# Eleven of twenty tile transposes from TensorE to VectorE and DMA, in a two-layer kernel

## The chip, the cores and the metric

One Trainium2 chip; the kernel runs on one of its cores. The metric is the device time of one execution in microseconds. Three runs of the kernel before took 754.48, 754.50 and 754.84, median 754.5. The profile is of one further execution of the same program.

## The reference

The input is `x` of shape (4, 512, 256), all in float32. Two layers follow each other; each normalizes and adds two branches to its input:

```python
xn = _layernorm(x, axis=-1)
x = x + _L0_attn_ref(xn, ...) + _L0_ffn_ref(xn, ...)
xn = _layernorm(x, axis=-1)
x = x + _L1_attn_ref(xn, ...) + _L1_ffn_ref(xn, ...)
```

The first branch of layer 0 is an mLSTM block with its own MLP. What matters here is its end (`_rmsnorm(x, w)` is `w * x * rsqrt(mean(x * x) + eps)` over the features):

```python
h_out = jax.nn.sigmoid(o_pre) * h_norm
x1 = x + h_out @ w_out
h2 = _rmsnorm(x1, norm2_w)
mlp = jax.nn.silu(h2 @ w_gate) * (h2 @ w_up) @ w_down
return x1 + mlp
```

The second branch of layer 0 is a gated FFN of 704 columns with eight low-rank experts, of which the router chooses two for each token. Layer 1 has causal attention over the first axis (four positions, 16 heads) and a gated FFN of 1024 columns whose hidden values are thinned to two of four.

## The kernel before, in words

The 512 positions are cut into four row blocks `j` = 0 to 3 of 128. A block with its four batch entries is a tile of 128 partitions by 4 x 256. A product contracts over the partitions, so whatever is multiplied with a weight over its 256 features must first lie with features on partitions: two halves `k` of 128 features, each with 4 x 128 tokens. Each such turn is one "tile transpose": `transposed` does one half `k` with four 128x128 TensorE transposes into a PSUM bank and one ScalarE eviction; a whole tile takes eight transposes and two evictions. Each row block has five of them, 20 in all:

- `front`: the normalized input of layer 0, into `xnT` (for block 0 `first_front` does it in pieces)
- `out`: the gated mLSTM output `sg`, into `hoT` (tile name `featT`), multiplied with `w_out`
- `second`: the second norm's result, into `h2T` (also `featT`); here the eviction multiplies with `norm2_w`
- `norm`: the normalized input of layer 1, in `front_rows`, into `xnT`
- `mixed`: the attention output `o` of layer 1, into `oT`, read by `finish_rows`

Layer 0 runs for each block `front`, `choice` and `routing` (which experts; `low` are the low-rank inputs), `mlstm`, `experts` (matmul outputs `chunk`, `acc`) and `mlp` (outputs `gp`, `up`, then `yp`). Layer 1 runs `attention_rows`, `attend_rows`, `rows` (gate and up as products of a seven-product scheme, outputs `x`, `y`, `z`), `sparsified` and `finish_rows`.

These parts are generators. `Flow` interleaves them into one order while the program is built: a `Clock` holds an estimate of when each engine is free and each tile ready, and a generator that yields a time is continued when TensorE's estimated time has come there. The order so found is kept on every engine (`keep_in_program_order`); DMAs are all issued on SP's queue except for four loads at the start. In this plan a DMA counts 0.5 us for issue, a given time, and 2.0 until it has landed. The program that runs has no planner in it: each engine takes its instructions in that fixed order and waits for semaphores.

`mlstm(0)` scales `w_out` on POOL (GpSimd) before its first use. `inv_sqrt` is a power, also on POOL. In `mlstm` the per-head sums `ss` go through it, then VectorE multiplies `ss` with `den`, then POOL forms `sg` (tile name `qm`) from it with four operations.

All compute instructions go through the wrapper at line 225, so they carry that line in the profile and are told apart by tile names. DMAs carry line 330.

Of the kernel before, what the change touches and what calls it, by code (L numbers as in the profile page):

```python
# [13 lines left out]
P = 128  # L14
# [14 lines left out]
BANKS = 8  # L29
AHEAD = 4  # L30
LITTLE = 1.0


@with_exitstack
def layers_kernel(ctx: ExitStack, tc: tile.TileContext, io: dict, out: bass.AP):
# [440 lines left out]
                xn[:, b, :], x[:, b, :], mv[:, b, 0:1], rstd[:, b : b + 1], ALU.subtract, ALU.mult  # L476
            )

    def transposed(src, dst, k, scale=None):

        pt = mm_ps("pt")
        for i in range(B):
            transpose(pt[:, i * P : (i + 1) * P], src(i, k), ident)
        if scale is None:
            act.copy(dst[:, k, :], pt)
        else:
            act.mul(dst[:, k, :], pt, scale[:, k : k + 1])

    def project(ps, w, xT, lo, n):

        for k in range(KD):
            mm(ps[0:n, :], w[:, k, lo : lo + n], xT[:, k, :], start=(k == 0), stop=(k == KD - 1))

# [8 lines left out]
    def sides(w, rooms, by):  # L504
# [12 lines left out]
        def kept(n):  # L517
# [3 lines left out]
                "a22": lambda q: v[:, 1, q, 1, :], "s3": lambda q: v[:, 0, q, 1, :],  # L521
                "s1": kept(0), "s2": kept(1), "s4": kept(2)}

    def other_sides(xT, t, by):

        b11, b12, b21, b22 = (xT[:, k, h * HALF : (h + 1) * HALF] for k in range(2) for h in range(2))
        for n, a, b in ((0, b12, b11), (1, b22, t[:, 0, :]), (2, b22, b12), (3, b21, t[:, 1, :])):
            by.tensor_tensor(out=t[:, n, :], in0=a, in1=b, op=ALU.subtract)
        return {"b11": b11, "b21": b21, "b22": b22,
                **{f"t{n + 1}": t[:, n, :] for n in range(4)}}  # L530

# [87 lines left out]
    def front_rows(j, norm=None):  # L619

        xn = new(both, [P, B, D], "xn")
        yield from norm(x_sb[j], xn) if norm else layernorm(both, x_sb[j], xn)
        xT = new(both, [P, KD, S], "xnT")
        for k in range(KD):
            yield from flow.wait(xn, banks=1)
            transposed(lambda l, k: xn[:, l, k * P : (k + 1) * P], xT, k)
        yield from flow.wait(xT)
        xTs[j] = xT

    with ExitStack() as l0:  # L630
        wk0 = l0.enter_context(tc.tile_pool(name="l0", bufs=1))
# [37 lines left out]
        def front_tiles(j):  # L669
            xns[j] = new(both, [P, B, D], "xn")  # L670

            rrs[j] = new(sm, [P, 4, B], "rr", 2)
            vas[j] = new(wk0, [P, B, H, DV + 1], "va", 2), new(sm, [P, B, 2 * H], "gz", 2)
            return xns[j], rrs[j], *vas[j], new(both, [P, KD, S], "xnT"), new(sm, [P, B, E], "pr")

        def rms_of(rr, ms, va):

# [5 lines left out]
        def values(xnT, b):  # L683
            vp = mm_ps("vp")
            for k in range(KD):
                mm(vp[:, 0:V], xnT[:, k, cols_of(b)], wvg[:, k, :], start=(k == 0),
                   stop=(k == KD - 1))
            return vp

# [5 lines left out]
        def first_front():  # L695

            x = x_sb[0]
            xn, rr, va, gz, xnT, pr = front_tiles(0)
            stats = new(both, [P, B, 6], "stats", 2)
            mv = new(both, [P, B, 2], "mv", 2)  # L700
            rstd = new(both, [P, 2, B], "rstd2")
# [9 lines left out]
            def normed(b):  # L711
                dve.tensor_scalar(
                    xn[:, b, :], x[:, b, :], mv[:, b, 0:1], rstd[:, 1, b : b + 1], ALU.subtract,
                    ALU.mult)
                pt = mm_ps("pt")
                for k in range(KD):
                    transpose(pt[:, k * P : (k + 1) * P], xn[:, b, k * P : (k + 1) * P], ident)
                act.copy(xnT[:, :, cols_of(b)], pt[:, 0 : KD * P].rearrange(
                    "p (k t) -> p k t", k=KD))
                if b == 0:  # L720
                    keep_busy(4)
                    clock.let_go(idle)
# [50 lines left out]
        def front(j):  # L773

            xn, rr, va, gz, xnT, pr = front_tiles(j)
            ms = rr[:, 3, :]
            yield from layernorm(both, x_sb[j], xn, ms)
            inv_sqrt(rr[:, 0, :], ms)  # L780
            for k in range(KD):
                yield from flow.wait(xn, banks=1)
                transposed(lambda i, k: xn[:, i, k * P : (k + 1) * P], xnT, k)
            yield from flow.wait(rr)
            rms_of(rr, ms, va)
            for b in range(B):
                yield from flow.wait(xnT, rr, banks=1)
                vp = values(xnT, b)
                dve.tensor_copy(pr[:, b, :], vp[:, D + 2 * H : V])
                values_read(vp, b, rr, va, gz)  # L790
            xnTs[j] = xnT
            yield from flow.wait(pr)
            yield from choice(j, pr)
# [43 lines left out]
        def mlstm(j):  # L837
# [277 lines left out]
            if first:  # L1115
                for k in range(KD):
                    pool.tensor_scalar(
                        w_out[:, k, :], w_out[:, k, :], mh_c[:, k : k + 1], 0.5, ALU.mult,
                        ALU.mult)
            sg = new(wk0, [P, B, D], "qm")  # L1120
            for bp in range(0, B, 2):
                yield from flow.wait(banks=1)
                o_ps = mm_ps("o_ps")
                for b in (bp, bp + 1):
                    o = o_ps[:, (b - bp) * D : (b - bp + 1) * D]
                    for k in range(KD):
                        mm(o, xnT[:, k, cols_of(b)], w_og[:, k, :], start=(k == 0),
                           stop=(k == KD - 1))
                for b in (bp, bp + 1):
                    act.activation(  # L1130
                        sg[:, b, :], o_ps[:, (b - bp) * D : (b - bp + 1) * D], AF.Tanh,
                        scale=rr[:, 2, b : b + 1])
# [28 lines left out]
                    out=by_head(sg[:, b, :]), in0=hv[:, b, :, :],  # L1161
                    in1=ss[:, b, :].unsqueeze(2).to_broadcast([P, H, DV]), op=ALU.mult)

            hoT = new(wk0, [P, KD, S], "featT", 2)
            for k in range(KD):
                yield from flow.wait(sg, banks=1)
                transposed(lambda b, k: sg[:, b, k * P : (k + 1) * P], hoT, k)
            for bp in range(0, B, 2):
                yield from flow.wait(hoT, banks=1)
                yp = mm_ps("yp")  # L1170
                for b in (bp, bp + 1):
                    for k in range(KD):
                        mm(yp[:, (b - bp) * D : (b - bp + 1) * D], hoT[:, k, cols_of(b)],
                           w_out[:, k, :], start=(k == 0), stop=(k == KD - 1))
                x1 = xn[:, bp : bp + 2, :].rearrange("p b d -> p (b d)")
                dve.tensor_tensor(x1, yp, x1, ALU.add)
# [13 lines left out]
            yield from flow.wait(r2)  # L1190
            for b in range(B):
                act.mul(xn[:, b, :], xn[:, b, :], r2[:, b : b + 1])
            h2T = new(wk0, [P, KD, S], "featT", 2)
            for k in range(KD):
                yield from flow.wait(xn, banks=1)
                transposed(lambda i, k: xn[:, i, k * P : (k + 1) * P], h2T, k, norm2_c)
            yield from flow.wait(h2T)
            h2Ts[j] = h2T

        def add_down(xb, bp, terms):  # L1200

# [77 lines left out]
        def experts(j):  # L1279
# [23 lines left out]
            def products(ps, parts, step):  # L1303


                for m in range(2):
                    for k in range(KD if step == 0 else 1):
                        for r0, half, c in parts:
                            f0, n = FCH[c]
                            o = ps[r0 : r0 + n, m * T : (m + 1) * T]  # L1310
                            if step == 0:
                                mm(o, wguT[:, m, k, f0 : f0 + n], xnT[:, k, here(half)],
                                   start=(m == k == 0), stop=False, at_once=len(parts),
                                   skip_group_check=True)
                            else:
# [175 lines left out]

        def following(j):

            yield flow.soon(30)
            while j >= 2 and j - 2 not in attended:
                yield flow.soon()
            yield from front(j)
# [44 lines left out]
    with ExitStack() as l1:  # L1542
# [4 lines left out]
        def attend_rows(j, q, k, v):  # L1547
# [37 lines left out]
                    o[:, l, :], pd[:, 0:m, :].rearrange("p m c -> p c m"), AX.X, ALU.add)  # L1585
            while j >= 2 and j - 2 not in out_of:
                yield flow.soon()
            oT = new(wk1, [P, KD, S], "oT", 2)
            for k in range(KD):
                yield from flow.wait(o, banks=1)  # L1590
                transposed(lambda l, k: o[:, l, k * P : (k + 1) * P], oT, k)
            outs[j] = oT

        def sparsified(j, hs):

# [41 lines left out]
        def finish_rows(j):  # L1637
# [5 lines left out]

            while len(halves.get(j, ())) < 2 and j < NJ - 1 or j == NJ - 2 and not written:
                yield flow.soon()
            terms = [(oT[:, k, :], aoT[:, k, :]) for k in range(KD)]
            terms += [(a[:, n, :], f_down[:, 4 * i + n, :])
                      for i, a in enumerate(gated[j]) for n in range(4)]

            m = 1 if j == NJ - 1 else 2  # L1650
# [1 line left out]
            for n0, n1 in ((0, 2), (2, 6), (6, 10)):  # L1652
                for lp in range(0, B, m):
# [7 lines left out]
                    for l in range(lp, lp + m):  # L1661
                        yield 0
                        for n in range(n0, n1):

                            mm(yps[lp // m][:, (l - lp) * D : (l - lp + 1) * D],
                               terms[n][0][:, l * P : (l + 1) * P], terms[n][1],
                               start=(n == 0 and l == lp), stop=(n == 9 and l == lp + m - 1),
                               skip_group_check=True)
            out_of.add(j)
# [8 lines left out]
        def attention_rows(j):  # L1678
# [4 lines left out]
            for l in range(B):  # L1683
                for name, lo, n in (("qk_ps", 0 if l else D, 2 * D if l else D), ("v_ps", 2 * D, D)):
                    yield from flow.wait(xT, banks=1)
                    ps = mm_ps(name)
                    for kk in range(KD):
                        mm(ps[:, 0:n], xT[:, kk, l * P : (l + 1) * P], qkvT[:, kk, lo : lo + n],
                           start=(kk == 0), stop=(kk == KD - 1))
                    if lo < 2 * D:  # L1690
                        if l:
# [11 lines left out]

        bs = {}
        sevens = Sevens(room)
        mm(sevens.z, ident, xTs[0][:, 0, :], start=True, stop=True)

        def room_of_sides():
            return new(wk1, [P, 4, HALF], "xd", 2)
# [148 lines left out]
```

## Time and profile before

| what | value |
|---|---|
| median of three runs | 754.5 us (754.48 to 754.84) |
| profiled execution: span from its first to its last instruction | 753.0 us; the page gives no other time of this execution |
| TensorE busy (matmul) | 746.1 us, 99% |
| VectorE busy | 482.1 us, 64% |
| ScalarE busy | 262.2 us, 35% |
| POOL busy | 173.9 us, 23% |
| transposes named `pt` | 160, of one pass each |
| evictions of `pt` | 0.59 us (plain), 0.68 us (with `norm_w`), 128x512 |
| DMA moved | 25.47 MB in 18961 packets |

By stretches, from the trace (us from the span's start; layer 1 begins at about 522):

| stretch | TensorE busy | VectorE | ScalarE | POOL |
|---|---|---|---|---|
| 0 to 60 | 57.50 | 44.59 | 22.02 | 24.28 |
| 60 to 170 | 109.55 | 76.50 | 37.35 | 26.34 |
| 170 to 280 | 109.65 | 67.99 | 32.31 | 25.87 |
| 280 to 400 | 119.76 | 67.82 | 33.61 | 22.04 |
| 400 to 520 | 120.00 | 63.93 | 27.87 | 20.94 |
| 520 to 640 | 119.81 | 85.17 | 69.67 | 40.52 |
| 640 to 753 | 109.87 | 76.15 | 39.39 | 13.93 |

A group's row reads: line, engine, operation, written tile, read tiles, shape, count, then busy us and mean ns of one, then the idle time before and what ended it. PE is TensorE's matmuls, DVE VectorE, ACT ScalarE. Durations of matmuls overlap, so what a matmul occupies is read from the distance between starts.

### The profile page before, as it was taken

To read this page: it belongs to the slowest core of one execution; us is meant where nothing else is said; L and a number is where in the kernel's file an instruction comes from. 1 tells how busy PE (TensorE), PEld (TensorE's weight loads), DVE (VectorE), ACT (ScalarE), POOL (GpSimd) and SP (SyncE) were. 2 spreads that over 40 slices of the span, in tenths; PEclk is the share of its full clock that TensorE was granted. 3 is DMA by queue.
4 is the path that set the end of the run, shared out by engine and by line. 5 is a ranking of instruction groups with operands and counts; after the bars stand their busy time and mean duration, and the time that the engine had idled before them with its cause. 6 is when DMAs were issued, how large, how long until landed. Compare 5 with 4: busy or idle time off the path is not lost.

```text
span 753.0 us, 10208 instructions
## 1 busy us (share of the span) xinstructions
PE 746.1 (99%) x3962; PEld 552.0 (73%) x3962; DVE 482.1 (64%) x1078; ACT 262.2 (35%) x569; POOL 173.9 (23%) x162
## 2 busy tenths in 40 slices
PE   9999999999999999999999999999999999999998
PEld 6787778766578776765777675655777778788887
DVE  5877586775743788644367745343269898698671
ACT  3334133433122433131233221211276874652510
POOL 6230052050132060203112023040141534520000
PEclk9999999999999999999999999999999999999999
DMA  7930000030000030000030210001000000000001
GB/s 237 300 113 0 3 0 1 3 112 0 1 2 1 3 111 1 1 1 1 0 114 1 112 44 14 1 0 56 1 1 0 2 0 1 29 0 29 1 15 42
DMA packets 18961, 25.47 MB, mean 34 GB/s; under 512 B 2784, under 2 KB 12768, under 8 KB 18912
## 3 DMA queue, kind: packets, MB, share of 16 engines
q1 hardware_dynamic: 17824, 24.53, 10.1%
q8 instruction: 31, 0.51, 0.3%
q10 hardware_dynamic: 1088, 0.28, 0.2%
q14 instruction: 18, 0.15, 0.1%
HBM read 22.65 MB, written 2.16 MB: 33 GB/s over the span
## 4 chain that ended last, share of the span: by engine, by line
PE 91%; DVE 6%; POOL 1%; ACT 1%; issue 1%; DMA 0%; POOLq 0%; DVEq 0%
PE chunk L225 18%; PE yp L225 16%; PE acc L225 11%; PE up L225 9%; PE gp L225 7%; PE x L225 6%; PE y L225 3%; PE qk_ps L225 3%; PE pt L225 2%; PE vp L225 2%; PE o_ps L225 2%; PE lp L225 2%; PE z L225 2%; PE v_ps L225 1%; PE qk L225 1%; PE sums L225 1%
## 5 line engine op out<-in xcount | busy, mean ns | idle before, releaser
L225 ACT ACTIVATE sl<-chunk 128x256 f32<-128x256 f32 x132 | 50.5, 383 | 122.3 <-PE chunk L225 106.6
L225 PE MATMUL chunk<-low,lora 128*128 128x256 f32 (+1 forms) x384 | 85.8, 383 | 1.6 <-DVE he_pair L225 1.1
L225 PE MATMUL chunk<-xnT,wguT 128*128 128x256 f32 (+1 forms) x384 | 83.2, 383 | 0.0
L225 PEld LDWEIGHTS chunk<-xnT,wguT 128*128 128x128 f32 (+1 forms) x384 | 64.2, 181 | 20.4 <-issue 8.8
L225 PEld LDWEIGHTS chunk<-low,lora 128*128 128x128 f32 (+1 forms) x384 | 63.7, 181 | 17.1 <-issue 5.1
L225 DVE SCALAR_TENSOR_TENSOR sl<-sl,chunk 128x256 f32<-128x256 f32 x132 | 54.7, 415 | 29.8 <-ACT sl L225 29.3
L225 PE MATMUL gp<-featT,w_gate 128*128 128x512 f32 x128 | 60.3, 593 | 0.0
L225 PE MATMUL up<-featT,w_up 128*128 128x512 f32 x128 | 60.3, 593 | 0.0
L225 PE MATMUL yp<-w_down,hid 128*128 128x256 f32 x256 | 56.6, 379 | 0.0
L225 PE MATMUL yp<-w_gate,hs 128*128 128x256 f32 x256 | 56.2, 379 | 0.0
L225 PEld LDWEIGHTS yp<-w_down,hid 128*128 128x128 f32 x256 | 48.4, 190 | 8.2 <-issue 1.9
L225 PEld LDWEIGHTS yp<-w_gate,hs 128*128 128x128 f32 x256 | 48.6, 190 | 6.6
L225 ACT ACTIVATE tmp<-gp 128x512 f32<-128x512 f32 x32 | 19.1, 597 | 91.3 <-PE gp L225 91.3
L225 DVE SCALAR_TENSOR_TENSOR tmp<-tmp,gp 128x512 f32<-128x512 f32 x32 | 22.0, 687 | 43.1 <-ACT tmp L225 43.0
L225 POOL TENSOR_TENSOR pd<-k,q 128x512 f32<-128x512 f32 (+2 forms) x12 | 27.8, 2321 | 92.0 <-ACT k L225 82.1
L225 POOL TENSOR_TENSOR ss<-ss,mhalf 128x32 f32<-128x32 f32 x4 | 22.0, 5501 | 101.4 <-DVE ss L225 101.4
L225 PEld LDWEIGHTS up<-featT,w_up 128*128 128x128 f32 x128 | 24.1, 190 | 27.6 <-issue 26.5
L225 PEld LDWEIGHTS gp<-featT,w_gate 128*128 128x128 f32 x128 | 24.0, 190 | 27.5 <-issue 26.8
L225 PE MATMUL acc<-WdT,hid 128*128 128x256 f32 (+1 forms) x192 | 41.1, 382 | 0.0
L225 PE MATMUL acc<-tmp,lora 128*128 128x512 f32 x80 | 40.4, 595 | 0.0
L225 PEld LDWEIGHTS acc<-WdT,hid 128*128 128x128 f32 (+1 forms) x192 | 32.8, 189 | 7.5 <-issue 3.2
L225 DVE TENSOR_TENSOR tmp<-chunk,sl 128x256 f32<-128x256 f32 x80 | 33.9, 424 | 2.8
(293 smaller groups left out, 1325.7 us busy)
## 6 DMA issues: line engine op xcount, KB each, us to landing
ct<-m_dram SPq DMA_DIRECT2D x8, 1024.0 KB, 8.0
x<-in_x SPq DMA_DIRECT2D x3, 512.0 KB, 10.0
out<-x SPq DMA_DIRECT2D x6, 256.0 KB, 2.1
w_gate<-in_w_gate SPq DMA_DIRECT2D x1, 1024.0 KB, 6.4
w_up<-in_w_up SPq DMA_DIRECT2D x1, 1024.0 KB, 7.4
w_down<-in_w_down SPq DMA_DIRECT2D x1, 1024.0 KB, 10.3
wguT<-in_f_gate SPq DMA_DIRECT2D x1, 1024.0 KB, 4.7
lora<-in_f_up SPq DMA_DIRECT2D x1, 1024.0 KB, 5.0
```

The costliest lines, as they stand in the source:

```text
L225: return tc.keep_in_program_order(f(*args, **kw))
```

## The change

A set `MOVED` names 11 of the 20 tile transposes. For these, one VectorE instruction turns every 32x32 block of the tile within its 32 partitions and writes the result to the new tile `t`; a DMA writes `t` to a DRAM tile `moved`; four DMAs read it back, one for each quarter of 32 partitions, so that the blocks come to the right partitions. The other nine stay on TensorE. The transposed tile's layout changes from (half, batch entry, token) to (batch entry, half, token) for all 20, and its readers take it through a view. The multiplication with `norm2_w` moves from the eviction into the weights: POOL multiplies `w_gate` and `w_up` with it once, in `mlstm(0)`. `following` waits 15 instead of 30 of the plan's microseconds before it starts the next block's `front`.

```diff
+MOVED = {('front', 1), ('front', 2), ('front', 3), ('mixed', 0), ('mixed', 2), ('mixed', 3), ('norm', 0), ('out', 0),
+         ('out', 1), ('second', 1), ('second', 3)}
...
-    def transposed(src, dst, k, scale=None):
-
-        pt = mm_ps("pt")
-        for i in range(B):
-            transpose(pt[:, i * P : (i + 1) * P], src(i, k), ident)
-        if scale is None:
-            act.copy(dst[:, k, :], pt)
-        else:
-            act.mul(dst[:, k, :], pt, scale[:, k : k + 1])
+    Q = 32
+    NQ = P // Q
+
+    def turned(src, t):
+
+
+        dve.transpose(
+            t.rearrange("p (m q i) -> p m q i", m=NQ, i=Q),
+            src.rearrange("p l (k m i) -> p m (l k) i", m=NQ, i=Q))
+        n = t.shape[1] // NQ
+        moved = new(dram, [NQ * P, n], "moved")
+        dma(moved.rearrange("(m p) x -> p m x", p=P), t.rearrange("p (m x) -> p m x", x=n), 1.6)
+        for m in range(NQ):
+            dma(t[m * Q : (m + 1) * Q, :].rearrange("i (q a j) -> i q a j", a=NQ, j=Q),
+                moved[m * P : (m + 1) * P, :].rearrange("(a i) (q j) -> i q a j", i=Q, j=Q), 0.6)
+
+    def turned_by(what, j, src, t):
+
+        yield from flow.wait(src)
+        if (what, j) in MOVED:
+            turned(src, t)
+            return
+        for l in range(B):
+            if l % 2 == 0:
+                yield from flow.wait(banks=1)
+                pt = mm_ps("pt")
+            for k in range(KD):
+                i = l % 2 * KD + k
+                transpose(pt[:, i * P : (i + 1) * P], src[:, l, k * P : (k + 1) * P], ident)
+            if l % 2:
+                act.copy(t[:, (l - 1) * KD * P : (l + 1) * KD * P], pt)
+
+    def by_token(t):
+        return t.rearrange("p (l k t) -> p k l t", l=B, k=KD)
...
@@ mlstm, for the first block
                     pool.tensor_scalar(
                         w_out[:, k, :], w_out[:, k, :], mh_c[:, k : k + 1], 0.5, ALU.mult,
                         ALU.mult)
+                    for w in (w_gate, w_up):
+                        pool.tensor_scalar(
+                            w[:, k, :], w[:, k, :], norm2_c[:, k : k + 1], None, ALU.mult)
...
@@ mlstm, second norm; the other four places change in the same way
-            h2T = new(wk0, [P, KD, S], "featT", 2)
-            for k in range(KD):
-                yield from flow.wait(xn, banks=1)
-                transposed(lambda i, k: xn[:, i, k * P : (k + 1) * P], h2T, k, norm2_c)
-            yield from flow.wait(h2T)
-            h2Ts[j] = h2T
+            t = turned_tile(wk0, "featT", 2)
+            yield from turned_by("second", j, xn, t)
+            yield from flow.wait(t)
+            h2Ts[j] = by_token(t)
...
@@ following
-            yield flow.soon(30)
+            yield flow.soon(15)
```

## The prediction

> **What bounds the kernel now.** I read the page's busy times and its slices first, then the chain that ended last.
>
> ```profile
> span 753.0 us, 10208 instructions
> ...
> PE 746.1 (99%) x3962; PEld 552.0 (73%) x3962; DVE 482.1 (64%) x1078; ACT 262.2 (35%) x569; POOL 173.9 (23%) x162
> ...
> PEclk9999999999999999999999999999999999999999
> ...
> PE 91%; DVE 6%; POOL 1%; ACT 1%; issue 1%; DMA 0%; POOLq 0%; DVEq 0%
> ```
>
> TensorE is busy in every slice at the full granted clock, and no other engine comes near it. The waits of TensorE itself (columns: total us, times, longest) leave almost nothing:
>
> ```profile
> PE idle L225 <- POOL ident masks.py:199: 1.5, 1, 1.5
> PE chunk L225 <- DVE he_pair L225: 1.1, 2, 0.9
> PE chunk L225 <- DVE ss L225: 0.4, 1, 0.4
> PE pt L225 <- DVE xn L225: 0.3, 1, 0.3
> PE pt L225 <- DVE o L225: 0.2, 1, 0.2
> ```
>
> So TensorE's own work sets the end: what is taken from it is gained one for one, and every wait that it newly meets is lost one for one. What the eight transposes of a tile occupy is seen in the timeline (start, duration, engine):
>
> ```profile
> 474.62 1.04 PE L225 MATMUL pt<-ident,xn 128*128 128x128 f32 x8
> 475.32 1.26 ACT L225 ACTIVATE featT<-pt,norm_w 128x512 f32<-128x512 f32 x2
> 475.50 1.02 PE L225 MATMUL up<-featT,w_up 128*128 128x512 f32 x2
> ```
>
> Eight transposes start at 474.62 and the next matmul at 475.50: 0.88 us, 0.109 each, although one lasts 0.27. They are one pass each; a 128x256 matmul is two passes 0.216 apart, a 128x512 one two passes 0.429 apart.
>
> **The gain.** 11 tiles x 8 transposes x 0.109 = 9.6 us leave TensorE. The upper bound is the pitch averaged with the gaps around transposes, 0.121, which makes 10.6. 22 evictions (0.59 or 0.68 us, ACT 35% busy) also go; nothing waits for ACT there once the transposes are gone. I take 9.6.
>
> **What takes their place, per tile:** one VectorE transpose of 128x1024, a write to DRAM of 512 KB in 512 pieces of 1 KB, then, when this has landed, four reads of 128 KB in 1024 pieces of 128 B, all on SP's queue.
>
> VectorE transpose: not in this trace. Nearest rows for 1024 f32 elements are the TENSOR_TENSOR `ct<-ct,by_pos` and the dense reduce, both 1.22 at best; below lies 0.68 (1024 bf16), above 1.94 (a strided reduce). I take 1.25: 11 x 1.25 = 14 us more on an engine that is 64% busy.
>
> Write and reads, from the SP queue and the landing times:
>
> ```profile
> 148.17 0.32 SPq L330 DMA_DIRECT2D m_dram<-by_row  x1
> 150.12 0.91 SPq L330 DMA_DIRECT2D ct<-m_dram  x2
> ```
>
> This pair is the same hop in small: a write, and a read that waits for it, issued 1.95 us later. The write's 32 packets ran for 0.18 of it, so 1.8 is fixed. In the DMA packet records 512 packets of 1 KB (two `out<-x` stores) ran in 1.63 us. Write to first read: 1.8 + 1.6 = 3.4. For the reads: the first packet of `ct` came 1.0 after its issue; the wait on it ended 0.5 after its last packet. Packets of 32 B last 9 ns and of 512 B 27 ns; a straight line between gives 12.6 ns for 128 B, so 256 packets on each of 16 engines take 3.2. Reads: 1.0 + 3.2 + 0.5 = 4.7. The hop is 8.1 at a steady flow. Lower bound: packets at the 9 ns price, 7.2. Upper bound: each read costs an issue as long as the longest of this queue (`lora<-in_AdT`, 3.19; that one stood in a full queue) or a packet of 50 ns, about 18. The four short `AdT` and `WdT` loads, 64 partitions each, were issued in 0.59, 0.60, 1.59 and 3.19, ordinary ones in 0.37; the reads have odd shapes too, so I add 0.8 for issue: 8.9.
>
> [...] If a 128 B piece cost as much as a 512 B one the sum would be the one of the first rival. [...]
>
> **Where the hop lies.** The order of the changed program says, for each moved tile, the last TensorE instruction that anything ahead of the VectorE transpose needs (its queue included), and the first matmul that reads the result. Between them TensorE has this work, at the pitches above: front(1) 12.9 us (24 chunk, 3 acc), out(0) 11.3, front(2) 15.7, out(1) 14.1 (16 yp, 22 chunk, 12 of them half), front(3) 13.6, second(3) 13.8 (32 yp x 2 x 0.216), second(1) 31, norm(0) 22, and mixed 58, 74 and 41. From this go the instructions up to the transpose, the transpose, and the hop. second(3): evacuation of `up` 0.9, VectorE and ACT up to the last xn 2.1, transpose 1.25, hop 8.1 = 12.4; margin 1.4. front(1): VectorE's queue (four xn of 0.64, then four chunk operations of 0.42) is through 3.0 after the last chunk, 1.25, 8.1: 12.4; margin 0.5. out(1): a store of `x` 0.9, the power of `ss` on POOL 0.4 later, `ss` 0.2, four qm 2.34, 1.25, 8.1: 13.2; margin 0.9. front(3) 2.5, front(2) 3.0, the rest over 10. With the hop at 8.9 front(1) is late by 0.3 and nothing else: +0.3. With it d longer than 8.1 the six tight tiles lose sum(max(0, d - margin)).
>
> SP's queue holds the `m_dram` and `ct` transfers and the stores of `out`; the new DMAs stand behind these in time order, and for the first three blocks `ct` (packets over 8.2 us) is through about 2 us before the next moved write. What is queued behind a moved tile on SP is next needed 20 us later or more. VectorE's transpose waits for nothing that isn't nearly there, except in out(0).
>
> **The fold of norm2.** Four POOL multiplications of 128x1024. Rows:
>
> ```profile
> L225 POOL TENSOR_SCALAR w_og<-w_og,norm_w 128x256 f32<-128x256 f32 x2 | 1.8, 922 | 3.4 <-DMA w_og<-in_w_og 3.4
> L225 POOL TENSOR_SCALAR wq<-wq,norm_w 128x128 f32<-128x128 f32 x2 | 1.2, 601 | 0.0
> L225 POOL TENSOR_SCALAR w_out<-w_out,mh_w 128x256 f32<-128x256 f32 x2 | 1.0, 522 | 0.0
> ```
>
> 601 and 922 ns make 0.28 + 2.5 ns an element: 2.85 us for 1024, 11.4 for four. Bounds: w_out's rate 2.1 each (8.4), w_og's 3.7 (14.8). In the profile POOL idled 39 us before the copy `tmp<-rank` (96.1); but in the changed order the scalings stand behind that copy and ahead of `low`, of the 5.5 us power of `ss` and of qm. So: last qk matmul at 76.3 of TensorE's work, four `ct<-qk,ct` 2.5, rank 0.7, POOL copy 0.6, w_out 1.0, scalings 11.4, `low` 2 x 1.56, power 5.5: 101.1. On VectorE the product with `ss` waits for this, and behind it are queued two pairs for chunks, 0.2 + 4 x 0.42: 103.0. TensorE needs the second at 101.0: 2.0 us of wait, where it lost 0.4 before (`chunk <- ss`): +1.6, bounds 0 and +5. out(0) itself, then at 103.6 + 1.25 + 8.1 = 113.0 against 112.3 + 2.0, keeps a margin of 1.3.
>
> **The rest.** `following` starts 15 us earlier: same instructions. Reads of the new layout have runs of 128 elements; the page's 128x256 and 128x512 matmuls have one duration whatever their operand; no price, bounds 0 to +2 for the re-planned order as a whole. Removed waits on pt (0.3 + 0.2) are in the 10.6.
>
> Sum: 753.0 - 9.6 + 0.3 + 1.6 = 745.3 span. The page gives this execution no time but its span; the median of the runs, 754.5, is 1.5 above, so 746.8.
>
> **Rivals.**
> (a) Slower: the 128 B reads. For: no row has them, and every tight tile is planned within 3 us. At a price of 27 ns (the 512 B packet) they take 6.9 instead of 3.2, d = 3.7 (issue hidden under it): 3.2 + 2.4 + 2.8 + 2.3 + 1.2 + 0.7 = 12.6 of waits; 753 - 9.6 + 1.6 + 12.6 = 757.6, 759.1 as a run. The change turns at d = 2.9, a hop of 11.0 us, or 24 ns a packet. At 50 ns (d = 9.6) the same sum gives 48 of waits, 794. Against: 32 B packets at 9 ns.
> (b) Nothing new is waited for, POOL included (its quick rate): 753.0 - 10.6 = 742.4, run 743.9. For: the tight margins are all positive by the steady hop.
> (c) POOL is the wait: 14.8 us of scalings and VectorE held 5 us: 753.0 - 9.6 + 5 + 0.3 = 748.7, run 750.2.
> (d) VectorE becomes the limit: 482 + 14 of 745 is 67%; only its bursts matter. A transpose at 1.94 adds 0.7 to d, about +0.7.
>
> **How the numbers follow.** Forecast 0.42, (b) 0.15, (c) and (d) 0.13, (a) 0.30, of which a third ends far above 760 and a tenth near no change. 754.5 x 0.2% = 1.5 us is about what can be told from no change. Faster: 0.42 + 0.15 + 0.13 - 0.01 = 0.69; same 0.04; slower 0.27. The range starts at (b), 743.5, and reaches into (a) to 764 (d = 4.5, 17.4 of waits), leaving out about 0.17 above and below.
>
> **What would show it.** Right: transposes of `pt` fall from 160 to 72; TensorE busy about 736; VectorE gains 11 rows near 1.25; the write lands in 3.4 and each read within 5; TensorE's waits list shows the DMA's tiles with under 1 us and `chunk <- ss` near 2. Wrong: waits of TensorE on `xnT` or `featT` DMAs of 2 us and more at vp, yp and gp; reads issued in over 0.7 us each; packets of 128 B well above 13 ns; POOL rows of over 3.5 us ahead of the power.

## The result, and the profile after

The changed kernel took 758.7 us (median of four, 756.9 to 759.6), the kernel before 754.5 beside it: a ratio of 1.0053, 95% interval 1.0039 to 1.0068. It is slower by 0.5%, where 1% faster was forecast. The profiled execution has a span of 757.9 against 753.0; it is the slowest of the four.

The page of the changed kernel (busy times, granted clock by slices, the chain by engines, DMA issues):

```profile
span 757.9 us, 10126 instructions
...
PE 742.9 (98%) x3874; PEld 545.1 (72%) x3874; DVE 493.4 (65%) x1089; ACT 250.2 (33%) x547; POOL 183.6 (24%) x166
...
PEclk9989999999999999999999999999999999999999
...
PE 84%; DVE 6%; DMA 4%; POOL 3%; SPq 2%; issue 1%; ACT 0%; ACTq 0%; DVEq 0%; POOLq 0%
...
moved<-xnT SPq DMA_DIRECT2D x4, 512.0 KB, 2.9
xnT<-moved SPq DMA_DIRECT2D x16, 128.0 KB, 3.7
```

The 88 matmul instructions are gone (3962 to 3874), but TensorE's busy time fell by 3.2 us only, and one early slice was not at the full clock. TensorE's waits (total us, times, longest) say where to look:

```profile
PE chunk L227 <- DVE hid L227: 4.6, 1, 4.6
PE chunk L227 <- DVE he_pair L227: 2.7, 2, 1.9
PE x L227 <- DVE w_down L227: 2.7, 1, 2.7
PE idle L227 <- POOL ident masks.py:199: 1.5, 1, 1.5
```

None of the new waits is for a tile that a DMA brings. There are three, and all are for VectorE: those on `hid` and `w_down`, and the longer one of the two on `he_pair` (the other, 0.9, is there before too). The DMA in the chain's shares lies before 46.65, in the loads and in `m_dram<-by_row` and `ct<-m_dram`; no moved tile is on the chain.

To get the whole account, I took for every matmul the distance to the next start and subtracted the usual distance after a matmul of its shape. The sum of what is left over is 50.3 us in the changed kernel and 35.9 before: 14.4 more. With the 9.6 us of transposes that left, this is +4.8, and the spans differ by 4.9. Three places make 15.0 of it; over all the rest the changed kernel has 0.6 less than the kernel before:

| place | wait beyond the usual pitch | matmuls at double pitch behind it | together, more than before |
|---|---|---|---|
| 46.9, `chunk`, waits for `hid` | 4.8 | 2.5 | 7.3 |
| 114.8, `chunk`, waits for `he_pair` | 2.0 (0.6 before) | 1.7 | 3.1 |
| 653.6, `x`, waits for `w_down` | 2.9 | 1.7 | 4.6 |

**First place.** The timeline of the changed kernel (start, duration, engine; in brackets the idle time before and what ended it):

```profile
44.10 2.01 POOL L227 TENSOR_SCALAR_AFFINE_SELECT ct<-ct 128x2048 f32<-128x2048 f32 x1 [10.09 <-DMA ct<-m_dram]
46.65 2.00 POOL L227 TENSOR_SCALAR_AFFINE_SELECT ct<-ct 128x2048 f32<-128x2048 f32 x1 [0.55 <-DMA ct<-m_dram]
48.63 1.03 POOL L227 TENSOR_TENSOR rstd<-rstd,mhalf 128x4 f32<-128x4 f32 x1
...
49.70 1.38 DVE L227 TENSOR_SCALAR xn<-x,mv,rstd 128x256 f32<-128x256 f32 x4 [7.43 <-POOL rstd L227]
...
51.44 0.42 DVE L227 TENSOR_TENSOR hid<-chunk,sl 128x256 f32<-128x256 f32 x1
...
51.92 3.78 PE L227 MATMUL chunk<-low,lora 128*128 128x256 f32 x8 [4.62 <-DVE hid L227]
...
52.57 1.23 DVE L227 STREAM_TRANSPOSE xnT<-xn 128x1024 f32<-128x1024 f32 x1
```

Read it from below. TensorE waits for `hid`. `hid` is late because `xn` of the next block stands ahead of it in VectorE's queue, and `xn` waited 7.43 us for `rstd`, with VectorE idle. That is a 1.03 us power on POOL, and ahead of it on POOL stand the two masks of `ct`, which wait for DMA. In the kernel before, the same masks ran at the same time, but `rstd` was only needed 5 us after them:

```profile
43.85 2.01 POOL L225 TENSOR_SCALAR_AFFINE_SELECT ct<-ct 128x2048 f32<-128x2048 f32 x1 [9.76 <-DMA ct<-m_dram]
46.41 2.00 POOL L225 TENSOR_SCALAR_AFFINE_SELECT ct<-ct 128x2048 f32<-128x2048 f32 x1 [0.54 <-DMA ct<-m_dram]
53.65 1.04 POOL L225 TENSOR_TENSOR rstd<-rstd,mhalf 128x4 f32<-128x4 f32 x1 [5.23 <-DVE rr L225]
```

So the cause is `following` with 15 instead of 30, which brought `xn` forward; not the moved tile, whose transpose comes after. And the planner had not wanted it so: it puts the power ahead of the masks. The run f1 below, which keeps that order, has the power at 40.29 and the masks at 44.02 and 46.56. In the program as built the masks overtook it. `affine_select` traces two instructions, a register move and the mask (for block 0 the changed kernel's trace has the moves at 31.55 and 44.07, 0.03 us each, and the masks at 44.10 and 46.65); the wrapper pins the returned one, the mask, behind the instruction traced just before it, which is the register move, and the register move is pinned to nothing. Where the text on the kernel before says that the order found is kept on every engine, this is the exception.

**Second place.** The four POOL scalings of `w_gate` and `w_up` (2.84 us each) run ahead of `low` and the power of `ss`, as predicted.

```profile
101.22 2.84 POOL L227 TENSOR_SCALAR w_gate<-w_gate,norm_w 128x1024 f32<-128x1024 f32 x1
104.04 2.84 POOL L227 TENSOR_SCALAR w_up<-w_up,norm_w 128x1024 f32<-128x1024 f32 x1
...
109.61 5.45 POOL L227 TENSOR_TENSOR ss<-ss,mhalf 128x32 f32<-128x32 f32 x1
...
117.01 1.08 PE L227 MATMUL chunk<-low,lora 128*64 128x256 f32 x8 [1.87 <-DVE he_pair L227]
```

**Third place.** The 1.24 us transpose of tile mixed(2) was put into VectorE's queue at 643.20, ahead of a run of comparisons. What followed is larger than 1.24 us. The changed kernel:

```profile
646.08 1.72 POOL L227 TENSOR_TENSOR pd<-k,q 128x512 f32<-128x512 f32 x1 [7.24 <-ACT k L227]
...
646.59 2.36 DVE L227 TENSOR_TENSOR rest<-hm 128x512 bf16<-128x512 f32 x2
...
648.66 1.96 POOL L227 TENSOR_TENSOR pd<-k,q 128x768 f32<-128x768 f32 x1 [0.86 <-ACT k L227]
...
648.87 2.29 DVE L227 TENSOR_TENSOR t<-c,c 128x1024 bf16<-128x1024 bf16 x1
...
656.63 1.22 PE L227 MATMUL x<-xd,wguT 128*128 128x256 f32 x4 [2.70 <-DVE w_down L227]
...
657.64 3.53 PE L227 MATMUL qk_ps<-WdT,xnT 128*128 128x512 f32 x4
```

The kernel before:

```profile
643.35 1.28 DVE L225 TENSOR_TENSOR rest<-hm 128x512 bf16<-128x512 f32 x2
...
644.55 0.68 DVE L225 TENSOR_TENSOR t<-c,c 128x1024 bf16<-128x1024 bf16 x1
...
645.19 7.17 POOL L225 TENSOR_TENSOR pd<-k,q 128x512 f32<-128x512 f32 x2 [8.55 <-ACT k L225]
```

In the kernel before VectorE went through at 1.28 and 0.68 us and POOL's two products took 7.17 (5.39 and 1.82); in the changed one POOL's products took 1.72 and 1.96 and VectorE's same instructions 2.36 and 2.29. Beside each other one of the two engines took longer, and the later order turned round which. VectorE lost 2.7 us on top of its 1.24.

In the changed kernel the first `rest` (1.76 of the 2.36) began 0.51 us after POOL's first product and ended 0.55 after its end, and `t` began 0.21 after the second product and ended 0.54 after its end.

**The clock.** Behind all three waits, matmuls start at twice their usual distance: the four `qk_ps` above take 3.53 us instead of 1.88. The windows of the changed kernel show the granted clock (the column PEclk, after the five engines' busy times):

```profile
47.00:50.00 3.00, 0.31 (x2) 0.00 (x0) 0.30 (x1) 0.38 (x1) 3.00 (x3) 1.00 0.00 0
50.00:53.00 3.00, 1.08 (x3) 0.90 (x4) 2.93 (x9) 0.00 (x0) 0.79 (x1) 0.50 0.00 0
```

The clock was at half from 49.98 to 56.81, from 118.25 to 121.66 and from 657.55 to 660.96.

### The profile page after: what moved, and what is told of

Same layout as the page of the kernel before. It is cut to its first block, busy times and chain, and to the rows that moved or that the text cites. A ratio compares the mean times of both kernels' runs of the same rounds, so it can differ in the third digit from the quotient of the medians.

```text
span 757.9 us, 10126 instructions
## 1 busy us (share of the span) xinstructions
PE 742.9 (98%) x3874; PEld 545.1 (72%) x3874; DVE 493.4 (65%) x1089; ACT 250.2 (33%) x547; POOL 183.6 (24%) x166
## 4 chain that ended last, share of the span: by engine, by line
PE 84%; DVE 6%; DMA 4%; POOL 3%; SPq 2%; issue 1%; ACT 0%; ACTq 0%; DVEq 0%; POOLq 0%
PE chunk L227 17%; PE yp L227 16%; PE acc L227 10%; PE up L227 9%; PE gp L227 7%; PE x L227 6%; PE y L227 3%; PE qk_ps L227 2%; SPq L332 2%; PE z L227 2%; PE vp L227 1%; PE o_ps L227 1%; PE lp L227 1%; DMA ct<-m_dram 1%; PE qk L227 1%; PE v_ps L227 1%
## 5 line engine op out<-in xcount | busy, mean ns | idle before, releaser
L227 ACT ACTIVATE sl<-chunk 128x256 f32<-128x256 f32 x132 | 50.3, 382 | 162.0 <-PE chunk L227 149.6
L227 PE MATMUL chunk<-low,lora 128*128 128x256 f32 (+1 forms) x384 | 87.6, 388 | 7.4 <-DVE hid L227 4.6
L227 PE MATMUL chunk<-xnT,wguT 128*128 128x256 f32 (+1 forms) x384 | 85.3, 388 | 0.0
L227 PEld LDWEIGHTS chunk<-xnT,wguT 128*128 128x128 f32 (+1 forms) x384 | 65.2, 184 | 21.5 <-issue 10.1
```

The costliest lines, as they stand in the source:

```text
L227: return tc.keep_in_program_order(f(*args, **kw))
```

## The experiments

Theory Q: the gain of 9.6 us is there, and three waits in the queues of VectorE and POOL, with the half clock behind them, eat it. Rival H: those waits only cover waits for the hop through DRAM. Rival L: the new layout or the re-planned order as such costs the time, all over the kernel.

An edit can make the planner choose another order for all that follows, and then compares two orders rather than one cause. f1 to f5 and g1 therefore tell the planner the same as the changed kernel does, and only issue the instruction in another place: in their traces TensorE, ScalarE and VectorE have the changed kernel's order, but for the one turn that is held back on purpose, and POOL has it but for the masks, the scalings and g1's zeros. g2, g4 and h2 are planned anew, and so, against its intent, is h1.

**One wait at a time, and all three.**

f1_select_in_order: the masks keep the planner's place.

```diff
+                with tc.issue_after(self.last) if name == "affine_select" else ExitStack():
+                    ins = f(*args, **kw)
+                self.last = ins.ins
-                return tc.keep_in_program_order(f(*args, **kw))
+                return tc.keep_in_program_order(ins)
```

> The changed kernel with one thing mended: GpSimd's two masks of block 0 (ct<-ct, each waiting for its ct DMA) keep the place that the planner gave them, behind the power of rstd; before, they ran ahead of it. Theory Q (the gain was eaten by three waits in VectorE's and GpSimd's queues, none of them on the DMA through DRAM): the wait of TensorE at 47 us (4.8 us over the usual pitch) and the 2.5 us lost at half clock after it both go: span 757.9 - 7.3 = 750.6, granted clock 1.00 in the first 60 us, VectorE's xn near 42 instead of 49.7. Rival H (the queue wait only covers a wait for the moved tile): the same microseconds come back as a wait of vp on xnT, span above 756. Rival L (new layout or re-planned order as such): less than 1 us changes.

Measured: span 751.4, 752.0 us as a run, ratio to the kernel before 0.9963 (0.9952 to 0.9974). The wait at 47 and the half clock behind it are gone, 7.3 us as expected; pinning also the first mask of block 2 put it behind four `wv` products and cost two new waits of 0.6 near 294 and 299.

f2_fold_early: the scalings are issued where POOL idles.

```diff
@@ front(1), behind inv_sqrt(rr[:, 0, :], ms)
+            if j == 1:
+                for k in range(KD):
+                    for w in (w_gate, w_up):
+                        tc.keep_in_program_order(nc.gpsimd.tensor_scalar(
+                            w[:, k, :], w[:, k, :], norm2_c[:, k : k + 1], None, ALU.mult))
@@ mlstm(0), there now for the planner only
-                        pool.tensor_scalar(
-                            w[:, k, :], w[:, k, :], norm2_c[:, k : k + 1], None, ALU.mult)
+                        clock.issue("pool", "tensor_scalar", (
+                            w[:, k, :], w[:, k, :], norm2_c[:, k : k + 1], None, ALU.mult), {})
```

> The changed kernel, order of all else kept, with the four norm2 scalings of w_gate and w_up issued on GpSimd right behind front(1)'s powers (near 51 us, where GpSimd idles 42 us) instead of ahead of low and the power of ss. Theory Q: only the wait at 114.8 us goes, 2.0 us: span 755.9. If the prediction's working is right, the power of ss starts when VectorE has made ss (near 107) instead of at 109.6, and its answer is no longer the last. Rival L: no change. A loss is possible if GpSimd's 11.4 us near 51 hold up VectorE's two-input operations there: up to 3 us.

Measured: span 756.2, run 757.3, ratio 1.0035 (1.0023 to 1.0047). The wait at 114.8 falls from 2.0 to 0.6, what the kernel before has, and the half clock behind it goes: 3.1 us. The span gains only 1.7 of them, mostly because the first wait came out 0.5 longer in this execution, with 0.6 more behind it at half clock.

f3_mixed2_later: the turn of mixed(2) is held back.

```diff
@@ turned, for mixed(2) only
-        dve.transpose(...)
+            later(key, "dve", "transpose", *args)
...
+                held[key].append(lambda to=to, of=of: nc.sync.dma_start(out=to, in_=of))
@@ attend_rows, behind the sum of scores
+                if j == 3 and l == 2:
+                    release("mixed")
```

> The changed kernel, order of all else kept, with the turn of tile mixed(2) on VectorE and its hop issued some 13 us later, behind the second sum of scores of block 3 (its reader yp comes 40 us after). Theory Q: VectorE is 1.24 us less late at 646; if GpSimd's products pd then no longer slip in between VectorE's two-input operations, all 2.7 us of held-up time go too: the wait of 2.9 us at 653.6 and the 1.7 us at half clock after it go, span 753.3. If they slip in all the same, the wait falls to 1.6 and the clock may stay up: 755. Rival L: no change.

Measured: span 752.1, run 755.0, ratio 1.0000 (0.9991 to 1.0008). The wait at 653.6 and the half clock behind it are gone, 4.6 us. The rest of the 5.8 goes with the first wait, which came out 0.9 shorter in this execution and left the clock at half for 3.4 us instead of 6.8.

f4_all_three: f1, f2 and f3 together.

> The three edits together, full computation. Theory Q: 757.9 - 7.3 - 2.0 - 4.6 = 744.0 span, some 744.8 as a run, 1.3% under the kernel before: the prediction's sum (745.3) without its terms for waits. Rival H: waits of TensorE on xnT, featT or oT of 1 us and more appear, span 748 and above. Rival L: above 755.

Measured: span 750.2, run 752.9, ratio 0.9973 (0.9962 to 0.9984). A miss by 6 us, and none of the theories had it. Its waits and POOL's timeline:

```profile
PE chunk L228 <- DVE hid L228: 4.5, 1, 4.5
```

```profile
50.67 2.84 POOL L840 TENSOR_SCALAR w_up<-w_up,norm_w 128x1024 f32<-128x1024 f32 x1
53.47 3.96 POOL L228 TENSOR_SCALAR_AFFINE_SELECT ct<-ct 128x2048 f32<-128x2048 f32 x2
```

The two edits do not fit together: f2 places the scalings behind `rstd`, f1 places the masks behind `rstd` too, and the masks came to stand behind 11.4 us of scalings. VectorE's `ct<-ct,by_pos` waited for them. It is the first wait once more, with other names.

f5_all_three_b: the scalings behind the masks of block 0, and only these two masks pinned.

```diff
@@ mlstm, behind the loop of the two affine_select
+            if first:
+                for k in range(KD):
+                    for w in (w_gate, w_up):
+                        tc.keep_in_program_order(nc.gpsimd.tensor_scalar(
+                            w[:, k, :], w[:, k, :], norm2_c[:, k : k + 1], None, ALU.mult))
```

> The three edits together again, but with the four norm2 scalings behind the two masks of block 0 instead of ahead of them (in the run before, the masks stood 11.4 us behind them and VectorE's ct waited, 4.6 us of TensorE), and with only the masks of block 0 pinned. Full computation. Theory Q: all three waits and both stretches at half clock go and nothing takes their place: span 757.9 - 7.3 - 2.0 - 4.6 = 744.0, 744.8 as a run, a ratio of 0.987. Rival H (the hop through DRAM is next in line once the queues are mended): waits of TensorE on xnT, featT or oT over 1 us each, span 747 and above. Rival L: above 750.

Measured: span 743.2, run 744.9 (744.5 to 745.0), ratio 0.9871 (0.9854 to 0.9887). The page's busy times and clock:

```profile
span 743.2 us, 10124 instructions
...
PE 736.9 (99%) x3874; PEld 542.1 (73%) x3874; DVE 493.2 (66%) x1089; ACT 250.5 (34%) x547; POOL 187.4 (25%) x166
...
PEclk9999999999999999999999999999999999999999
```

Its waits:

```profile
PE idle L230 <- POOL ident masks.py:199: 1.5, 1, 1.5
PE chunk L230 <- DVE he_pair L230: 1.3, 2, 0.9
PE acc L230 <- DVE tmp L230: 0.2, 1, 0.2
```

The left-over distances sum to 35.6, as in the kernel before (35.9). So the 9.6 us of transposes are gained in full, all else of the change is free in this order, and rivals H and L fall. (757.9 less the table's 15.0 is 742.9; theory Q's 744.0 left out the clock behind the second wait.) This kernel beats both.

**What causes the waits.**

g1_no_read: POOL's two products at the third place do not read.

```diff
+                if j == 3 and l < 3:
+                    tc.keep_in_program_order(nc.gpsimd.memset(pd[:, 0:m, :], 0.0))
```

> The changed kernel with GpSimd's first two products pd<-k,q of block 3 replaced by writes of zeros of the same size (their scores are left out); they read nothing, wait for nothing of ScalarE and run before VectorE's comparisons. If VectorE's rest<-hm (1.76 us instead of 0.68) and t<-c,c (2.29 instead of 0.68) were held up by these products, both fall to 0.68, VectorE is 2.7 us earlier, the wait at 653.6 shrinks from 2.9 to about 0.2 and the half clock behind it goes: span 753.4. If the 1.24 us transpose alone is the cause, nothing changes: 757.9, rest and t at 1.8 and 2.3.

Measured: span 751.4, run 754.6, ratio 0.9997 (0.9987 to 1.0006). VectorE's timeline:

```profile
641.07 1.24 DVE L227 STREAM_TRANSPOSE oT<-o 128x1024 f32<-128x1024 f32 x1
...
644.46 1.29 DVE L227 TENSOR_TENSOR rest<-hm 128x512 bf16<-128x512 f32 x2
645.67 0.68 DVE L227 TENSOR_TENSOR t<-c,c 128x1024 bf16<-128x1024 bf16 x1
```

The transpose is still there, and TensorE's wait on `w_down` is gone from its list of waits. So the 2.7 us that POOL's products held VectorE up are what made the 1.24 us transpose into a wait. The zeros also run 7 to 8 us earlier than the products did, counted from VectorE's transpose, so this run shows `rest` and `t` at 1.29 and 0.68 us with no work of POOL beside them, against 2.36 and 2.29 with it; what in that work holds them up was not shown. (The 2.0 us beyond the expected 753.4 go with the clock: behind the first two waits, which are both still there, it was at half for 3.4 us in all, where the changed kernel has 6.8 and 3.4.)

g2_before_start15: the kernel before with the earlier start alone.

```diff
-            yield flow.soon(30)
+            yield flow.soon(15)
```

> The kernel before with one part of the change alone: the next block's front starts 15 us after the block instead of 30. GpSimd's two masks run ahead of the power of rstd here too. Theory Q: the wait near 47 us and the half clock behind it come with this part alone: 753.0 + 7.3 = 760.3 span, less what the plan gains or loses elsewhere (under 2 us). Rival (the wait needs the turned tile): 753 to 754.

Measured: span 761.4, run 763.2, ratio 1.0113 (1.0098 to 1.0128). Its timeline has the same chain, with TensorE's own transpose at the end of it:

```profile
48.37 1.04 POOL L225 TENSOR_TENSOR rstd<-rstd,mhalf 128x4 f32<-128x4 f32 x1
...
49.44 1.38 DVE L225 TENSOR_SCALAR xn<-x,mv,rstd 128x256 f32<-128x256 f32 x4 [7.48 <-POOL rstd L225]
...
50.00 2.21 PE L225 MATMUL pt<-ident,xn 128*128 128x128 f32 x8 [5.59 <-DVE xn L225]
```

The wait needs no moved tile. One number in the diff brought it: 5.8 us beyond the usual pitch and 2.0 at half clock, where the whole run lost 8.4.

g4_dose: nine waits of graded length in the kernel before.

```diff
+                n = DOSE.get((j, f))
+                if n:
+                    ...
+                    mm(ps[:, 0:P], ones, ident, start=True, stop=True)
+                    dve.tensor_copy(one, ps[:, 0 : B * H])
+                    pool.tensor_tensor(out=two[:, 0:n], in0=one[:, 0:n], in1=mhalf[:, 0:n], op=ALU.pow)
+                    mm(ps[:, 0:n], ident, two[:, 0:n], start=True, stop=True)
```

> The kernel before with nine waits of TensorE of graded length put in ahead of gate projections: a 128x128 matmul, a copy on VectorE, a power of n columns on GpSimd, a matmul that reads it. By the rows of the power (1.03 us for 4 columns, 5.5 for 32) and 0.9 for the rest: n = 4, 6, 8, 10, 12, 14, 16, 20, 24 make waits of some 1.9, 2.2, 2.6, 2.9, 3.2, 3.5, 3.8, 4.5, 5.1 us. Theory T (a wait over a length between 2.0 and 2.7 always halves the clock for 3.4 us or more): all from 2.6 on lose 1.7 to 2.5 us behind the wait, those under it nothing. Theory W (activity is judged over fixed stretches of 3.4 us, so it depends on how the wait lies in them): waits of 2 to 3.4 us fall on either side, from about 5 on the clock always falls.

Measured: the waits came out between 2.2 and 5.6 us, not in the order of n, since other work on VectorE and POOL stood ahead of some. In the changed kernel's trace the three stretches of half clock are 6.83, 3.41 and 3.41 us long and begin at 49.98, 118.25 and 657.55; the starts lie 68.27 and 539.31 us apart, 20 and 158 times 3.413. So I divided the traces into fields of 3.413 us on such a grid and summed TensorE's idle time in each. In the changed kernel the four fields ahead of a half-clock field have 2.68 and 1.94 (first place), 1.87 (second) and 2.49 us (third) of it. In g4 the windows around the waits have a mean granted clock of 1.00, of 0.83 to 0.87 over 10 to 13 us (one field at half) or of 0.69 over 11 us (two):

| wait beyond the pitch (us), start | idle time in the fields it touches | clock behind it |
|---|---|---|
| 2.6, 184.8 | 1.1 and 1.5 | full |
| 2.2, 566.9 | 1.3 and 1.0 | full |
| 2.2, 213.0 | 1.95 in one | half for 3.4 us |
| 2.9, 498.9 | 1.0 and 1.9 | half for 3.4 us |
| 3.5, 533.3 | 2.7 in one | half for 3.4 us |
| 5.0, 313.8 | 1.9 and 3.1 | half for 3.4 us |
| 5.1, 549.4 | 1.8 and 3.3 | half for 3.4 us |
| 4.4, 473.4 | 2.6 and 1.9 | half for 6.8 us |
| 5.6, 361.0 | 2.3 and 3.2 | half for 6.8 us |

A wait of 2.2 us halved the clock, and one of 2.6 did not; in h1 below a wait of 3.4 us, 1.6 and 1.8 in its two fields, did not either. Of the waits named here, those with 1.87 us or more of idle time in one field were followed by half clock, and those with up to 1.8 in each were not. Not every such field counted for itself: at 313.8 fields with 1.9 and 3.1 gave 3.4 us at half clock, at 473.4 fields with 2.6 and 1.9 gave 6.8. The rows fit theory W and not theory T, and no field ahead of half clock that is named here was idle as a whole.

**How near the hop is.**

h1_hop_longer: f5 with one more copy of each moved tile in DRAM.

```diff
+        first = moved
+        moved = new(dram, [NQ * P, n], "again")
...
+                (moved[:, :], first[:, :], None)]
```

> The mended kernel (all three edits, span 743.2), same order, with one more copy DRAM to DRAM of the 512 KB between the write and the reads of every moved tile; the planner does not know of it. It makes the hop longer by d: 1.8 us fixed and 1.6 for its packets by the prediction's rows, 3.4, up to 5 if the copy moves slower. Margins from the mended run (next reader on TensorE, less the issue of the last read, less 3.1 to 3.7 to land): out(0) 0.3, out(1) 1.0, front(1) 1.2, second(3) 1.5, front(2) and front(3) 2.8, the others over 6. Theory Q with the prediction's table of margins: each loses d less its margin; 3.1 + 2.4 + 2.2 + 1.9 + 0.6 + 0.6 = 10.8 at d = 3.4, 20.4 at d = 5, and up to 1.7 more behind each wait of some 2 us for the clock: span 754 to 770, waits of TensorE for DMA at vp, yp and gp. If the hop is hidden as a whole: 743 to 744.

Measured: span 780.8, run 782.6, ratio 1.0378 (1.0363 to 1.0394), above all that was expected. The copy made the hop longer by 3.9 to 4.1 us. The waits:

```profile
PE vp L231 <- DMA xnT<-again: 13.6, 3, 5.2
PE yp L231 <- DMA featT<-again: 6.0, 1, 6.0
PE yp L231 <- issue: 4.6, 1, 4.6
PE gp L231 <- DMA featT<-again: 2.3, 1, 2.3
```

The row with "issue" is out(0), whose wait the profile gives no releaser. The six tight tiles are the ones that wait, and only they. But d less the margins at d = 4 is 14.4, and the waits beyond the usual pitch sum to 27.4; the clock adds some 10.

The difference is in the edit: the order is not the same. The planner isn't told that a DMA writes `again`, so for it the reads need not wait until a write has landed, and it counts the moved tiles as ready too early. In five of the six it put the reader further forward. front(2) in f5, then in h1:

```profile
165.60 1.13 PE L230 MATMUL acc<-he_pair,lora 64*128 64x512 f32 x4
...
169.78 3.94 PE L230 MATMUL vp<-wvg,xnT 128*128 128x280 f32 x16
```

```profile
185.37 6.00 PE L231 MATMUL vp<-wvg,xnT 128*128 128x280 f32 x16 [5.14 <-DMA xnT<-again]
...
194.74 1.13 PE L231 MATMUL acc<-he_pair,lora 64*128 64x512 f32 x4
```

Between the issue of the write and the first matmul that reads the tile, TensorE has this work at the usual pitches, in f5 and in h1:

| tile | f5 | h1 | d less its margin, plus the difference | wait measured |
|---|---|---|---|---|
| front(1) | 10.1 | 7.3 | 5.6 | 5.4 |
| out(0) | 9.3 | 7.6 | 5.4 | 4.7 |
| front(2) | 11.0 | 6.9 | 5.3 | 5.3 |
| out(1) | 8.2 | 6.5 | 4.7 | 6.1 |
| front(3) | 10.6 | 8.2 | 3.6 | 3.4 |
| second(3) | 9.5 | 9.5 | 2.5 | 2.4 |

The differences sum to 12.7, and 14.4 + 12.7 = 27.1. So the waits are d less the margins of the order that ran, within 0.7 for five tiles and 1.4 for out(1). What a longer hop costs in f5's own order no run shows; by the table it is an estimate of 14.4 and the clock behind it.

h2_mixed1_too: f5 with a twelfth tile.

```diff
-MOVED = {('front', 1),
+MOVED = {('mixed', 1), ('front', 1),
```

> The mended kernel with a twelfth tile moved, mixed(1) (68 us of TensorE's work between its VectorE transpose and its reader, so its hop is hidden); the planner re-plans from there on. By the price per tile that the mended run confirms (9.8 us for 11): 743.2 - 0.9 = 742.3, 744.0 as a run. Rival V (VectorE's queue is where these tiles are paid for, and each new order is a new throw): a wait of TensorE for VectorE of 1 to 5 us appears after 580, span 743.3 to 749.

Measured: span 744.1, run 746.0, ratio 0.9893 (0.9875 to 0.9910). No gain beyond f5 is seen: 0.9 us of transposes go, but the left-over distances sum to 37.4, 1.8 more than in f5, and TensorE newly waits for ScalarE.

```profile
PE x L230 <- ACT z L230: 1.4, 2, 1.1
```

A new throw of the order, as rival V had it, with the wait on another engine than it said.

## Why the prediction was wrong

The forecast was 746.8 and faster; measured 758.7 and slower. Step by step:

- **TensorE bounds, and what is taken from it is gained one for one.** Right. In the changed kernel its busy time fell only to 742.9, with the waits and the half clock in it; in f5 its busy time is 736.9 (about 736 predicted) and the span 743.2 is 9.8 less than before (9.6).
- **The VectorE transpose, 1.25.** Right: eleven rows of 1.23 to 1.25.
- **The hop, 8.9.** Right. In the changed kernel, from the write's issue to the first read's 2.9 to 3.1 us (3.4 predicted); the four reads are issued 0.6 to 0.8 apart; packets of 128 B lasted 13.2 ns in the mean of 45056 (12.6). The last of them ended 7.8 to 8.5 after the write's issue, over the eleven tiles. The issue of a read took 0.56 to 0.80, of the fourth 0.68 to 1.21; over 0.7 was named as a sign of being wrong, but no matmul waited for it. So rival (a), which needed 27 ns, did not happen; that its 759.1 is near 758.7 is chance, and the measured time lies in the range only by the part that was opened for it. By the changed kernel's packets, 128 B in 13.2 ns are 9.7 B a ns, 512 B in 27 ns (the median) 19: a piece of 128 B did not cost as much as one of 512 B, and the hop stayed hidden at half the rate.
- **The margins.** Right as a list: no moved tile is waited for in the changed kernel, and the six tight ones are those that h1 makes late. As a price list they hold too, once the order that h1 really ran is put in: 27.1 against 27.4 measured.
- **The fold of norm2, +1.6.** Right: 2.84 to 2.85 us a scaling (2.85), and the wait grew by 1.4 us. The clock behind it, 1.7, was not in it.
- **"`following` starts 15 us earlier: same instructions", "no price, bounds 0 to +2 for the re-planned order as a whole", and "VectorE's transpose waits for nothing that isn't nearly there, except in out(0)".** This is the step that failed, a term put at nothing: 7.3 us at front(1) and 4.6 at mixed(2), 11.9 where 0 to 2 was allowed. For front(1) the working began at VectorE's four `xn` and did not ask what `xn` waits for. Its power stood behind two masks on POOL that wait for DMA, in the changed program's own order on POOL; the rows of the masks (43.85 and 46.41) and of the power (53.65) were in the trace of before. That the turn was cheap was right; that `xn` was moved ahead of VectorE's other work while its power stood behind a DMA wait on another queue was not costed. For mixed(2) the working looked at what the turn waits for, and not at what waits behind the turn.
- **Rival (d), "only its bursts matter".** The right kind, but no burst was priced: its +0.7 is for a slower transpose. VectorE's 1.24 us in a burst cost 4.6 at mixed(2), since POOL then got in first (2.7) and the clock halved behind the wait (1.7).
- **Waits lost one for one.** Wrong: 5.9 of the 15.0 us are matmuls at half clock behind the waits. They came at 2.5, 1.7 and 1.7 behind waits of 4.8, 2.0 and 2.9 us; at the second, TensorE was idle for 1.87 us of the 3.41 ahead of half clock.

Together: 753.0 less 9.6 of transposes, plus 15.0 at the three places, less 0.6 elsewhere, is 757.8, against the 757.9 of the profile.

## What to carry to other kernels

When a kernel stands at 99% of one engine, an instruction taken off it can be gained in full, as f5 shows, but only as long as none of the in-order queues that feed it gets a new wait at its head: for every instruction that a change brings forward, list what it waits for, and then what stands ahead of that on the other engine's queue in the program as built, not in the plan. Price a new wait of TensorE at itself plus what half clock may take behind it: here 2.5 us behind the wait of 4.8, 1.7 behind those of 2.0 and 2.9, and nothing behind g4's of 2.2 (at 566.9) and 2.6. When the parts of a change work singly, put them together with the queues in hand again: f4 made the first wait anew out of two good edits, and f5 differs from it by the place of four POOL instructions and by leaving the later masks unpinned. And read the order of a variant from its trace before it is called the same: h1's wasn't.

## What the runs showed of the hardware that was not expected

- In the changed kernel half clock came in stretches of 3.41 and 6.83 us, with starts 20 and 158 times 3.413 us apart, and TensorE was idle for 1.87 us of the 3.41 ahead of the one at 118.25. Two waits of 2.2 us in g4 had different prices, 0 and 1.7 us. The spread of the runs goes with the granted clock: f3's eleven runs reach from a span of 750.6 at a mean of 0.998 to 753.9 at 0.993, and f5, with no half clock before TensorE's last matmul, keeps within 0.5 us.
- The same instructions of VectorE and POOL took different times in two orders: in the changed kernel VectorE's `rest` and `t`, begun 0.51 and 0.21 us after POOL's products, took 2.7 us longer than in the kernel before; there POOL's first product, begun 0.64 us after `t`, took 5.39 us instead of 1.72.
- In h1 a DRAM to DRAM copy of 512 KB lengthened a chain on one queue by 3.9 to 4.1 us; the write of 512 KB from SBUF, with the wait behind it, took 2.9 to 3.1.
